# Other buffers and banks for the last element's layers 1 to 3, and a list of positions on 8 elements per partition

## The chip, the cores and the metric

The kernel runs on one core of one Trainium2 chip. The metric is the device time of one execution in microseconds. Three runs of the kernel before took 14069.84, 14073.2 and 14090.67 us; the median is 14073.2 us.

## The reference, cut to what matters

Sixteen independent elements, each with 1024 nodes, 64 features and an adjacency matrix of 1024 by 1024, pass through four residual layers:

```python
h = jnp.maximum(_layernorm(x, axis=-1), 0.0)
x = x + _L0_gnn_ref(h, adj, nodemask, W1, b1, W2, b2)   # dilated neighbours, three quantiles of their features, MLP
h = jnp.maximum(_layernorm(x, axis=-1), 0.0)
x = x + _L1_gnn_ref(h, adj)                             # (adj + I) @ h / row sum
h = jnp.maximum(_layernorm(x, axis=-1), 0.0)
x = x + _L2_gnn_ref(h, adj, ...)                        # attention, 8 heads of 64; adj is a bias on the scores
h = jnp.maximum(_layernorm(x, axis=-1), 0.0)
x = x + _L3_gnn_ref(h, adj, weight, bias)               # adj @ (h @ W) + b
```

In layer 2, with `g0` and `g1` per row, the attention is

```python
attn = g0 * (q @ k.T * SCALE) + g1 * adj
out = softmax(attn) @ v @ W_proj.T + b_proj
```

Layer 0 needs, for each node and feature, order statistics over the node's neighbours. Everything is in float32 at the interface.

## The kernel before

All loops are unrolled when the program is built. A setup builds constants in a scratch pool (`scr`), among them `rev`, the numbers 0 to 1023, each with its ten bits reversed, in float16: an iota over N = 1024 columns, the same on every partition, then ten pairs of VectorE operations (L137 and L141), a cast (L143) and a write to DRAM (L145). It is read back, 128 partitions by 1024, once for every two elements, when `ranks` turns the record of a sorting network back into ranks (L528).

After the scratch pool is closed, the working pool is opened. Before the first element's layer 0 starts, its ranks and its dilated neighbours are made (`background(0)`).

The main stage is the generator `picks`: for each of 16 elements 96 steps (8 groups of features, 2 halves of the nodes, 6 order statistics). Each step has three wide compare and multiply operations on VectorE (L735, L737, L739) and matmuls with the selection tables on TensorE. Between them stands the next element's preparation. Layers 1 to 3 of an element (`rest`) can start only when its layer 0 is over, so they are interleaved with the layer 0 of the next element: every step of `picks` gives a credit of 0.42, and a piece of layers 1 to 3 is traced for each credit used up (`two, due`, L1148). After the last element's layer 0 no picks are left; the last loop of the function (L1153) lets layers 1 to 3 of the last element run alone, with what is left of layer 3 of the element before.

Instructions run on each engine in one order that is settled when the program is built. It need not be the order of the code: `adjoining` keeps a set of matmuls together, and the instructions of a layer can be placed ahead of earlier code where they are ready.

Buffers are kept by tags. In SBUF: `a4` (4 buffers of 4 KB a partition; layer 0's compares), `tb` (6; the tables cum, c1, c0), `q4` (2), `hT` (1; layer 0's sum z), `b4` (2; `s` of layer 2, one per head, and h2), `bt` (2; transposed blocks of layers 1 and 2, and the loads of layer 3), `adj` (3; rows of the adjacency matrix, 512 KB a load), `kT`, `qT`, `v2` (1 each). In PSUM every tag has two banks: `pa`, `pc`, `pb`, and `sp`, which is one tile of two banks.

Layer 1, for each of 8 blocks of 128 rows: load `ad`, row sums on ScalarE, transpose the block in `chunk_cols` (TensorE into `pcols`, a bank of `pb`; ScalarE copies it to `aT` in `bt`), write `aT` to DRAM for layer 3, multiply by h (`weighted`, banks of `pb`), divide and add.

Layer 2, for each of 4 pairs of heads: projections into kT, qT and v by way of `pb`; then for each of 8 row blocks: load `ad` and scale it on ScalarE; for each half t of the 1024 columns the scores of both heads (L1074) go into the tile `sp`, and VectorE adds them to `ad` into `s` with a running extreme `nm` (L1083); ScalarE takes the exponential in place with its sum; `chunk_cols` transposes it to `eT`; `ao` multiplies it by v (L1093), `pp` projects it (L1104), and VectorE adds both heads to the residual (L1106). pcols, ao, pp, two and po all take their turn in the two banks of `pb`.

Layer 3 reads the transposed blocks back (`aT3` in `bt`) and multiplies.

Of the kernel before, what the change touches and what calls it, by code (L numbers as in the profile page):

```python
# [8 lines left out]
F32 = mybir.dt.float32  # L9
BF = mybir.dt.bfloat16  # L10
HP = mybir.dt.float16
F8 = mybir.dt.float8e4
I32 = mybir.dt.int32
# [8 lines left out]
P = 128  # L22
# [14 lines left out]
def tile_preln_adj_stack(  # L37
# [30 lines left out]
    nc = tc.nc  # L68
# [13 lines left out]
    def a4(name, shape=(P, N), dt=F32):  # L82
        return sb.tile(list(shape), dt, tag="a4", bufs=4, name=name)
# [14 lines left out]
    def pa(name, shape=(P, 512), dt=F32):  # L98
        return ps.tile(list(shape), dt, tag="pa", bufs=2, name=name)
# [2 lines left out]
        return ps.tile(list(shape), dt, tag="pc", bufs=2, name=name)  # L102


    def b4(name, shape=(P, N), dt=F32):
        return sb.tile(list(shape), dt, tag="b4", bufs=2, name=name)

    def pb(name, shape=(P, 512), dt=F32):
        return ps.tile(list(shape), dt, tag="pb", bufs=2, name=name)

    def small(name, shape, dt=F32, bufs=3):
# [6 lines left out]
    def sc(name, shape=(P, P), dt=F32):  # L118
        return scrp.tile(list(shape), dt, name=name)
# [7 lines left out]
    identh = const.tile([P, P], HP, name="identh")  # L127
    nc.vector.tensor_copy(identh, identf)

    rev_i = sc("rev_i", (P, N), I32)  # L130
    nc.gpsimd.iota(rev_i, pattern=[[1, N]], base=0, channel_multiplier=0)
    rev_a = sc("rev_a", (P, N), I32)
    rev_b = sc("rev_b", (P, N), I32)
    nc.vector.memset(rev_a, 0)
    for b_ in range(N.bit_length() - 1):
        up = N.bit_length() - 2 - 2 * b_
# [2 lines left out]
            op1=OP.logical_shift_left if up >= 0 else OP.logical_shift_right,  # L139
        )  # L140
        nc.vector.tensor_tensor(rev_a, rev_a, rev_b, OP.bitwise_or)  # L141
    rev = sc("rev", (P, N), HP)
    nc.vector.tensor_copy(rev, rev_a)  # L143
    rev_d = dram.tile([P, N], HP, name="rev_d")
    nc.sync.dma_start(rev_d, rev)  # L145
    not_i = const.tile([P, P], BF, name="not_i")
    nc.vector.tensor_scalar(not_i, identf, -1.0, 1.0, op0=OP.mult, op1=OP.add)
# [257 lines left out]

    def chunk_cols(ad, name):

        aT = sb.tile([P, C, P], F32, tag="bt", bufs=2, name=name)
        for s in range(2):
            pt = pb("pcols", (P, 4, P))  # L410
            adjoining(
                nc.tensor.transpose(pt[:, c, :], ad[:, (4 * s + c) * P : (4 * s + c + 1) * P], identf)  # L412
                for c in range(4)
            )
            nc.scalar.copy(aT[:, 4 * s : 4 * s + 4, :], pt)  # L415
        return aT
# [65 lines left out]
    def ranks(V):  # L482

        L = N.bit_length() - 1
        F = V
        steps = []
        for l in range(L):
            for k in range(l, -1, -1):
                steps.append((l, k))
        half = N // 2

        def sides(X, l, k):  # L500

            st = 1 << (L - 1 - k)
            v = X.rearrange("p (u two s) -> p u two s", two=2, s=st)
            lo, hi = v[:, :, 0, :], v[:, :, 1, :]
            return lo, (hi[:, ::-1, :] if k == l else hi), hi

        def like(X, k):
            return X.rearrange("p (u s) -> p u s", s=1 << (L - 1 - k))

        md = dram.tile([(len(steps) + 1) // 2, P, 2, half], HP, name="md")  # L510
        for n, (l, k) in enumerate(steps):
            G = q4("sv")
            lo, hi, _ = sides(F, l, k)
            olo, _, ohi = sides(G, l, k)
            if n % 2 == 0:
                m = b2_("sm", (P, 2, half), HP)
            nc.vector.tensor_tensor(like(m[:, n % 2, :], k), lo, hi, OP.is_gt)
            nc.vector.tensor_tensor(olo, lo, hi, OP.min)
            nc.vector.tensor_tensor(ohi, lo, hi, OP.max)
            if n % 2 == 1 or n == len(steps) - 1:  # L520
                nc.sync.dma_start(md[n // 2, :, : n % 2 + 1, :], m[:, : n % 2 + 1, :])
            F = G
            yield
        vs = dram.tile([P, N], F32, name="vs_d")
        nc.sync.dma_start(vs, F)
        yield "half"
        R = b2_("rev", (P, N), HP)
        nc.sync.dma_start(R, rev_d)  # L528

        last = (len(steps) - 1) // 4  # L530

        def fetch(i):
            m = q4("sb", (P, 4, half), HP)
            w = min(4, len(steps) - 4 * i)
            for s in range(0, w, 2):
                u = min(2, w - s)
                nc.sync.dma_start(m[:, s : s + u, :], md[2 * i + s // 2, :, :u, :])
            return m

        back = [fetch(i) for i in range(last, last - 2, -1)]  # L540
        for n in range(len(steps) - 1, -1, -1):
            l, k = steps[n]
            if n % 4 == 3 or n == len(steps) - 1:
                m = back.pop(0)
            G = b2_("sr", (P, N), HP)
            lo, _, hi = sides(R, l, k)
            olo, ohi, _ = sides(G, l, k)
            d = sb.tile([P, half], HP, tag="sd", bufs=1, name="sd")
            nc.vector.tensor_tensor(like(d, k), hi, lo, OP.subtract)
            nc.vector.tensor_tensor(d, d, m[:, n % 4, :], OP.mult)  # L550
            nc.vector.tensor_tensor(olo, lo, like(d, k), OP.add)
            nc.vector.tensor_tensor(ohi, hi, like(d, k), OP.subtract)
            R = G
            if n % 4 == 0 and n >= 8:
                back.append(fetch(n // 4 - 2))
            yield
        pt = pb("pr", (P, C, P), HP)
        adjoining(
            nc.tensor.transpose(pt[:, j, :], R[:, j * P : (j + 1) * P], identh) for j in range(C)
        )  # L560
        rs = b2_("rs", (P, C, P), HP)
        nc.scalar.copy(rs, pt)
        rk = dram.tile([P, C, P], HP, name="rk_d")
        nc.sync.dma_start(rk, rs)
        yield rk, vs
# [451 lines left out]
    def layer2(b, xr):  # L1017
# [17 lines left out]
        HW = H * D  # L1035
        for pr in range(H // 2):

            kT = sb.tile([P, N], F32, tag="kT", bufs=1, name="kT")
            qT = sb.tile([P, N], F32, tag="qT", bufs=1, name="qT")
            v = sb.tile([P, C, P], F32, tag="v2", bufs=1, name="v2")  # L1040
            for t in range(NH):
                hs = slice(t * 512, (t + 1) * 512)
                both = ((kT, slice(0, D), pb("pk")), (qT, slice(D, P), pb("pq")))
# [19 lines left out]
            for i in range(C):  # L1063
                ad = adj_rows(b, i)
                act(ad, ad, AF.Copy, scale=gm[:, i, 1:2])
                sums = small("sums", [P, 2])
                eTs = []
                ss = [b4("s") for _ in range(2)]
                nms = [None, None]
                for t in range(NH):  # L1070
                    hs = slice(t * 512, (t + 1) * 512)
                    sps = ps.tile([P, 2, 512], F32, tag="sp", bufs=1, name="sp")
                    adjoining(
                        nc.tensor.matmul(  # L1074
                            sps[:, e, :], qT[e * D : (e + 1) * D, i * P : (i + 1) * P],
                            kT[e * D : (e + 1) * D, hs], start=True, stop=True,
                        )
                        for e in range(2)
                    )
                    for e in range(2):  # L1080

                        nm = small("nm", [P, 1], bufs=6)
                        nc.vector.tensor_tensor_reduce(  # L1083
                            ss[e][:, hs], sps[:, e, :], ad[:, hs], -1.0, 3.0e38 if t == 0 else nms[e],
                            op0=OP.add, op1=OP.min, accum_out=nm,
                        )
                        nms[e] = nm
                for e in range(2):
                    act(ss[e], ss[e], AF.Exp, bias=nms[e], scale=-1.0, accum_out=sums[:, e : e + 1])
                    eTs.append(chunk_cols(ss[e], "eT"))  # L1090
                ao = pb("ao", (P, P))
                adjoining(
                    nc.tensor.matmul(  # L1093
                        ao[e * D : (e + 1) * D, :], v[:, j, e * D : (e + 1) * D], eTs[e][:, j, :],
                        start=j == 0, stop=j == C - 1, tile_position=(0, e * D), skip_group_check=True,
                    )
                    for j in range(C) for e in range(2)
                )
                rs = small("rs", [P, 2])
                nc.vector.reciprocal(rs, sums)  # L1100
                aT = small("aoT", [P, P], bufs=2)
                nc.scalar.copy(aT, ao)
                pp = pb("pp", (P, 2, D))
                nc.tensor.matmul(pp, aT, wproj[:, pr], start=True, stop=True)  # L1104
                for e in range(2):
                    nc.vector.scalar_tensor_tensor(  # L1106
                        xr[:, i, :], pp[:, e, :], rs[:, e : e + 1], xr[:, i, :], op0=OP.mult, op1=OP.add
                    )
                yield 1.0
# [39 lines left out]
    for r in picks():  # L1149
        due += r  # L1150
        while due > 0.0:
            due -= next(two) or due
    for _ in two:  # L1153
        pass

# [33 lines left out]
```

## Time and profile before

| | us |
|---|---|
| median of three runs | 14073.2 |
| profiled execution, its own time | 14083.1 |
| profiled execution, span of the core | 14080.9 |
| TensorE busy, in the span | 12452.1 (88%) |
| VectorE busy | 12849.4 (91%) |
| ScalarE busy | 8198.1 (58%) |
| GpSimd busy | 25.0 (0%) |

The profiled execution has its own time, a little above the median. The span runs from the first to the last instruction of the core. Shares are over the whole span; stages with different limits lie in it, so they are read stage by stage. In the rows of a group, `out<-in` names the tiles, the count follows the x, then come the busy time, the mean duration in ns, and the time that the engine was idle just before, with what ended it. PEld is TensorE's loading of weights, which lies beside its matmuls.

### The profile page before, as it was taken

The page shows a single profiled execution, that of the slowest core. Times are in us where ns is not written, and L with a number is a line of the kernel's source. Part 1 is how long each engine was busy: PE and PEld are TensorE (multiplying, and loading weights), DVE is VectorE, ACT ScalarE, POOL GpSimd, SP SyncE. Part 2 cuts the span into 40 slices and gives each one's busy share as a digit, 9 for nine tenths or more (in the row PEclk, how much of TensorE's full clock was granted, in tenths as well). Part 3 has the DMA queues.
Part 4 walks back from the last instruction along what each step waited for, and adds up shares of the span by engine and source line. Part 5 has one row for each costly group of instructions (what it writes and reads, how often), then busy time and mean ns, then how long its engine had stood idle before and what let it go on. Part 6 is the DMA issues. An engine that isn't in the chain of part 4 may idle for free. (4 is left out here: it accounts for less than half of the span.)

```text
span 14080.9 us, 236134 instructions
## 1 busy us (share of the span) xinstructions
PE 12452.1 (88%) x94402; PEld 5955.5 (42%) x95489; DVE 12849.4 (91%) x23280; ACT 8198.1 (58%) x14170; POOL 25.0 (0%) x138
## 2 busy tenths in 40 slices
PE   1889989999899998999899998998989999999987
PEld 0224444444444444444444444444444444444444
DVE  9999999999999999999999999999989999988863
ACT  1446656566566665656566665665656566665655
POOL 0000000000000000000000000000000000000000
PEclk9999999999999999999999999999999999999999
DMA  3012121211212112121211212122121211202011
GB/s 95 28 35 65 47 82 49 77 55 51 77 47 84 49 55 71 53 79 50 70 57 55 76 49 78 49 66 66 48 76 50 71 61 53 82 25 62 26 58 55
DMA packets 478672, 838.40 MB, mean 60 GB/s; under 512 B 232448, under 2 KB 234624, under 8 KB 477568
## 3 DMA queue, kind: packets, MB, share of 16 engines
q1 hardware_dynamic: 477568, 823.24, 18.8%
q8 instruction: 747, 12.24, 0.4%
q14 instruction: 357, 2.92, 0.1%
HBM read 616.27 MB, written 206.83 MB: 58 GB/s over the span
## 5 line engine op out<-in xcount | busy, mean ns | idle before, releaser
L699 PE MATMUL pword<-valid,dw 128*128 128x512 fp8e4 x8192 | 1985.5, 385 | 141.6 <-DVE dw L665 101.3
L691 PE MATMUL pc<-valid,cw 128*128 128x512 fp8e4 x8192 | 1973.9, 381 | 26.0 <-DVE valid L479 13.9
L737 DVE TENSOR_TENSOR wa<-le,c 128x2048 f16<-128x2048 f16 x1536 | 1865.8, 1215 | 134.8 <-PE prep L751 119.6
L735 DVE TENSOR_TENSOR le<-cum,krow 128x2048 f16<-128x2048 f16 x1536 | 1863.6, 1213 | 16.5 <-PE val L751 16.4
L739 DVE TENSOR_TENSOR wb<-le,c 128x2048 f16<-128x2048 f16 x1536 | 1864.1, 1214 | 3.5 <-PE prep L751 3.3
L362 ACT ACTIVATE s<-s,nm 128x1024 f32<-128x1024 f32 x1024 | 1169.9, 1143 | 728.3 <-DVE nm L1083 727.0
L758 ACT COPY wi<-prep 128x512 f32<-128x512 f32 x1536 | 896.8, 584 | 943.3 <-PE prep L751 796.9
L362 ACT ACTIVATE hi<-pword,mid_c 128x512 f16<-128x512 f32 x1024 | 703.2, 687 | 1140.4 <-PE pword L704 1135.5
L1074 PE MATMUL sp<-kT,qT 64*128 64x512 f32 x4096 | 1168.8, 646 | 200.8 <-DVE nm L1083 192.5
L699 PEld LDWEIGHTS <-dw 128*128 128x128 bf16 x8192 | 763.5, 99 | 1262.6 <-DVE dw L665 228.0
L412 PE MATMUL pcols<-identf,s 128*128 128x128 f32 x8192 | 1156.1, 283 | 155.7 <-ACT s L362 74.7
L691 PEld LDWEIGHTS <-cw 128*128 128x128 bf16 x8192 | 764.5, 98 | 1085.4 <-issue 250.1
L412 PEld LDWEIGHTS pcols<-identf,s 128*128 128x128 f32 x8192 | 913.8, 143 | 627.1 <-ACT eT L415 238.8
L415 ACT COPY eT<-pcols 128x512 f32<-128x512 f32 x2048 | 1110.1, 593 | 85.2 <-PE pcols L412 83.3
L1093 PE MATMUL ao<-eT,v 128*64 128x128 f32 x16384 | 1079.9, 277 | 63.8 <-ACT eT L415 60.7
L751 PE MATMUL val<-le,tab 128*32 128x512 f16 x12288 | 1092.2, 388 | 47.7 <-DVE vs L779 30.4
L779 DVE SCALAR_TENSOR_TENSOR vs<-pz,vs 128x512 f32<-128x512 f32 x1536 | 1045.0, 680 | 65.4 <-PE pv L1057 14.9
L362 ACT ACTIVATE vs<-val 128x512 f32<-128x512 f32 x1536 | 927.1, 604 | 235.7 <-PE val L751 146.3
L1093 PEld LDWEIGHTS ao<-eT,v 128*64 128x64 f32 x16384 | 905.5, 137 | 317.3 <-ACT eT L415 212.6
L694 ACT CAST cum<-pc 128x512 f16<-128x512 f32 x1024 | 603.8, 590 | 719.0 <-PE pc L691 674.7
L751 PE MATMUL prep<-wb,sel_w 128*32 128x512 f16 x6144 | 642.5, 396 | 261.8 <-DVE wb L739 238.5
L362 ACT ACTIVATE c<-pword,mid_c 128x512 f16<-128x512 f32 x1024 | 711.2, 695 | 196.9 <-PE pword L681 182.7
(260 smaller groups left out, 19147.0 us busy)
## 6 DMA issues: line engine op xcount, KB each, us to landing
ad<-in_adj_dram SPq DMA_DIRECT2D x768, 512.0 KB, 3.6
adjT_d<-aT SPq DMA_DIRECT2D x128, 512.0 KB, 4.6
aT<-adjT_d SPq DMA_DIRECT2D x128, 512.0 KB, 3.7
md<-sm SPq DMA_DIRECT2D x216, 256.0 KB, 2.0
sb<-md SPq DMA_DIRECT2D x216, 256.0 KB, 2.9
rem_d<-rem SPq DMA_DIRECT2D x128, 256.0 KB, 2.0
left_d<-left SPq DMA_DIRECT2D x128, 256.0 KB, 2.6
left<-left_d SPq DMA_DIRECT2D x128, 256.0 KB, 3.8
```

Of the source, the lines that this page charges most:

```text
L362: nc.scalar.activation(out_, in_, func, **kw)
L412: nc.tensor.transpose(pt[:, c, :], ad[:, (4 * s + c) * P : (4 * s + c + 1) * P], identf)
L415: nc.scalar.copy(aT[:, 4 * s : 4 * s + 4, :], pt)
L691: nc.tensor.matmul(pc, cw[:, j, :], valid[:, j, hs], start=j == 0, stop=j == C - 1)
L699: nc.tensor.matmul(pw_, dw[:, j, :], valid[:, j, hs], start=j == 0, stop=False, skip_group_check=True)
L735: nc.vector.tensor_tensor(le, cum, bc(el.krow[q][:, None, hs], [P, 4, 512]), OP.is_le)
L737: nc.vector.tensor_tensor(wa, le, c0, OP.mult)
L739: nc.vector.tensor_tensor(wb, le, c1, OP.mult)
L751: nc.tensor.matmul(dst[32 * pp : 32 * pp + 32, :], w[pp], r[pp], start=i in (0, 3), stop=i in (2, 4), tile_position=(0, 32 * pp),)
L779: nc.vector.scalar_tensor_tensor(vs, pz, -191.0, vs, op0=OP.is_equal, op1=OP.mult)
L1074: nc.tensor.matmul(sps[:, e, :], qT[e * D : (e + 1) * D, i * P : (i + 1) * P], kT[e * D : (e + 1) * D, hs], start=True, stop=True,)
L1093: nc.tensor.matmul(ao[e * D : (e + 1) * D, :], v[:, j, e * D : (e + 1) * D], eTs[e][:, j, :], start=j == 0, stop=j == C - 1, tile_position ...
```

## The change

A list `alone` is empty while `picks` runs and gets an entry just before the last loop. From then on (the last element's layers 1 to 3, and what is left of layer 3 of the element before) tiles are taken from other tags:

- `b4` (s, h2) takes from `a4`, with 4 buffers in place of 2;
- `chunk_cols` puts the transposed blocks into `tb`, with 6 buffers in place of 2;
- `pb` takes from `pa` for everything but `pcols`, which keeps the two banks of `pb`;
- kT, qT and v of the odd pairs of heads take from `q4` (two buffers) and `hT`;
- the scores of the second half of the columns go into two tiles of `pc`, those of the first stay in `sp`.

In the setup, `rev` is made as 8 numbers on each of 128 partitions, written to DRAM as 1024 numbers in a row, and read back with that row repeated for 128 partitions.

```diff
--- before.py
+++ after.py
@@ -102,10 +102,14 @@
         return ps.tile(list(shape), dt, tag="pc", bufs=2, name=name)
 
 
+    alone = []
+
     def b4(name, shape=(P, N), dt=F32):
-        return sb.tile(list(shape), dt, tag="b4", bufs=2, name=name)
+        return a4(name, shape, dt) if alone else sb.tile(list(shape), dt, tag="b4", bufs=2, name=name)
 
     def pb(name, shape=(P, 512), dt=F32):
+        if alone and name != "pcols":
+            return pa(name, shape, dt)
         return ps.tile(list(shape), dt, tag="pb", bufs=2, name=name)
 
     def small(name, shape, dt=F32, bufs=3):
@@ -127,10 +131,10 @@
     identh = const.tile([P, P], HP, name="identh")
     nc.vector.tensor_copy(identh, identf)
 
-    rev_i = sc("rev_i", (P, N), I32)
-    nc.gpsimd.iota(rev_i, pattern=[[1, N]], base=0, channel_multiplier=0)
-    rev_a = sc("rev_a", (P, N), I32)
-    rev_b = sc("rev_b", (P, N), I32)
+    rev_i = sc("rev_i", (P, C), I32)
+    nc.gpsimd.iota(rev_i, pattern=[[1, C]], base=0, channel_multiplier=C)
+    rev_a = sc("rev_a", (P, C), I32)
+    rev_b = sc("rev_b", (P, C), I32)
     nc.vector.memset(rev_a, 0)
     for b_ in range(N.bit_length() - 1):
         up = N.bit_length() - 2 - 2 * b_
@@ -139,9 +143,9 @@
             op1=OP.logical_shift_left if up >= 0 else OP.logical_shift_right,
         )
         nc.vector.tensor_tensor(rev_a, rev_a, rev_b, OP.bitwise_or)
-    rev = sc("rev", (P, N), HP)
+    rev = sc("rev", (P, C), HP)
     nc.vector.tensor_copy(rev, rev_a)
-    rev_d = dram.tile([P, N], HP, name="rev_d")
+    rev_d = dram.tile([P, C], HP, name="rev_d")
     nc.sync.dma_start(rev_d, rev)
     not_i = const.tile([P, P], BF, name="not_i")
     nc.vector.tensor_scalar(not_i, identf, -1.0, 1.0, op0=OP.mult, op1=OP.add)
@@ -405,7 +409,10 @@
 
     def chunk_cols(ad, name):
 
-        aT = sb.tile([P, C, P], F32, tag="bt", bufs=2, name=name)
+        aT = (
+            tb(name, (P, C, P), F32) if alone
+            else sb.tile([P, C, P], F32, tag="bt", bufs=2, name=name)
+        )
         for s in range(2):
             pt = pb("pcols", (P, 4, P))
             adjoining(
@@ -525,7 +532,7 @@
         nc.sync.dma_start(vs, F)
         yield "half"
         R = b2_("rev", (P, N), HP)
-        nc.sync.dma_start(R, rev_d)
+        nc.sync.dma_start(R, rev_d.rearrange("(o p) c -> o (p c)", o=1).to_broadcast([P, N]))
 
         last = (len(steps) - 1) // 4
 
@@ -1035,9 +1042,13 @@
         HW = H * D
         for pr in range(H // 2):
 
-            kT = sb.tile([P, N], F32, tag="kT", bufs=1, name="kT")
-            qT = sb.tile([P, N], F32, tag="qT", bufs=1, name="qT")
-            v = sb.tile([P, C, P], F32, tag="v2", bufs=1, name="v2")
+            if alone and pr % 2:
+                kT, qT = q4("kT"), q4("qT")
+                v = sb.tile([P, C, P], F32, tag="hT", bufs=1, name="v2")
+            else:
+                kT = sb.tile([P, N], F32, tag="kT", bufs=1, name="kT")
+                qT = sb.tile([P, N], F32, tag="qT", bufs=1, name="qT")
+                v = sb.tile([P, C, P], F32, tag="v2", bufs=1, name="v2")
             for t in range(NH):
                 hs = slice(t * 512, (t + 1) * 512)
                 both = ((kT, slice(0, D), pb("pk")), (qT, slice(D, P), pb("pq")))
@@ -1069,10 +1080,14 @@
                 nms = [None, None]
                 for t in range(NH):
                     hs = slice(t * 512, (t + 1) * 512)
-                    sps = ps.tile([P, 2, 512], F32, tag="sp", bufs=1, name="sp")
+                    if alone and t % 2:
+                        sps = [pc_("sp") for _ in range(2)]
+                    else:
+                        sp = ps.tile([P, 2, 512], F32, tag="sp", bufs=1, name="sp")
+                        sps = [sp[:, e, :] for e in range(2)]
                     adjoining(
                         nc.tensor.matmul(
-                            sps[:, e, :], qT[e * D : (e + 1) * D, i * P : (i + 1) * P],
+                            sps[e], qT[e * D : (e + 1) * D, i * P : (i + 1) * P],
                             kT[e * D : (e + 1) * D, hs], start=True, stop=True,
                         )
                         for e in range(2)
@@ -1081,7 +1096,7 @@
 
                         nm = small("nm", [P, 1], bufs=6)
                         nc.vector.tensor_tensor_reduce(
-                            ss[e][:, hs], sps[:, e, :], ad[:, hs], -1.0, 3.0e38 if t == 0 else nms[e],
+                            ss[e][:, hs], sps[e], ad[:, hs], -1.0, 3.0e38 if t == 0 else nms[e],
                             op0=OP.add, op1=OP.min, accum_out=nm,
                         )
                         nms[e] = nm
@@ -1150,6 +1165,7 @@
         due += r
         while due > 0.0:
             due -= next(two) or due
+    alone.append(True)
     for _ in two:
         pass
```

## The prediction

> **What bounds the kernel now.** I read the slices of the page first, to find where the bound changes; then the busy time by stages; then, inside the last stage, the waits and one iteration of the timeline; last the groups of VectorE in the setup.
>
> The slices of the page:
> ```profile
> PE   1889989999899998999899998998989999999987
> DVE  9999999999999999999999999999989999988863
> PEclk9999999999999999999999999999999999999999
> ```
> One slice is 352 us. VectorE (DVE) is full from the first slice to slice 37, TensorE (PE) nearly so from slice 2 on. Slice 1 has VectorE alone at 9: nothing else works there, so what VectorE spends in the setup is on the path. In slices 39 and 40 VectorE falls to 6 and 3 and TensorE to 8 and 7: nothing is full there.
>
> Busy time by stages (columns: stretch, length, then busy us of PE, PEld, DVE, ACT, POOL, granted clock, DMA share, GB/s). The bounds are mine: the first compare of layer 0 stands near 350, its last near 13,620; the first score of the last element's layer 2 at 13,721, its last product at 14,040.
> ```profile
> 352.00:12800.00 12448.00, 11300.49 (x85717) 5341.04 (x86732) 11711.17 (x20905) 7423.94 (x12822) 20.09 (x112) 0.98 0.19 59
> 13622.00:13722.00 100.00, 74.08 (x522) 53.99 (x520) 32.22 (x110) 40.39 (x80) 1.06 (x7) 0.74 0.41 134
> 13722.00:14041.00 319.00, 241.49 (x1924) 153.60 (x1924) 111.19 (x352) 192.99 (x335) 0.00 (x0) 0.96 0.16 49
> 14041.00:14081.00 40.00, 26.30 (x168) 21.30 (x168) 6.50 (x21) 5.98 (x14) 0.00 (x0) 0.54 0.34 110
> 13842.21:13859.76 17.55, 13.41 (x118) 8.62 (x117) 6.95 (x22) 11.56 (x20) 0.00 (x0) 1.00 0.21 61
> ```
> The third row is layer 2 of element 15 alone: TensorE works 241.5 of 319 us, ScalarE 193, VectorE 111, so 77.5 us of TensorE's time are holes. The last row is two of its 32 row blocks: 8.78 us each, of which TensorE needs 6.7, ScalarE 5.8 and VectorE 3.5.
>
> Who waits in that stage (13,737 to 14,041; waiter, releaser, total us, times, longest):
> ```profile
> DVE s L1083 <- PE sp L1074: 68.3, 33, 5.8
> DVE s L1083 <- PE pcols L412: 47.9, 54, 2.1
> PE sp L1074 <- DVE nm L1083: 35.6, 32, 1.5
> ```
> and from the timeline of one block:
> ```profile
> 13846.96 1.13 PE L1074 MATMUL sp<-kT,qT 64*128 64x512 f32 x4 [1.30 <-DVE nm L1083]
> 13848.02 1.09 PE L412 MATMUL pcols<-identf,s 128*128 128x128 f32 x8
> 13849.15 0.69 DVE L1083 CUSTOM_DVE_ANT_0 s<-sp,ad 128x512 f32<-128x512 f32 x1 [0.44 <-PE pcols L412]
> 13850.59 0.69 DVE L1083 CUSTOM_DVE_ANT_0 s<-sp,ad 128x512 f32<-128x512 f32 x1 [0.74 <-PE pcols L412]
> 13851.35 1.13 PE L1074 MATMUL sp<-kT,qT 64*128 64x512 f32 x4 [0.79 <-DVE nm L1083]
> ```
> The scores of the next block are ready at 13848.1, but VectorE may write them into `s` only once the transposes (pcols) have read the last block's `s`: `s` has two buffers, one per head. And the second half of the scores (13851.35) waits until VectorE has emptied the first, as `sp` is one pair of banks. So the blocks hang in a loop: transposes, VectorE, scores, VectorE, exponential, transposes. No engine bounds this stage; two buffers do.
>
> The setup's VectorE groups before 39.3 us:
> ```profile
> L141 DVE TENSOR_TENSOR rev_a<-rev_a,rev_b 128x1024 int32<-128x1024 int32 x10 | 12.1, 1214 | 0.0
> L137 DVE TENSOR_SCALAR rev_b<-rev_i 128x1024 int32<-128x1024 int32 x10 | 6.8, 676 | 0.0
> ```
> Half of VectorE's first 39 us is this list of positions, and no wait stands before either group.
>
> **What the Trainium skill says.** "VectorE: DVE Perf Modes", section "The TRN2 errata — SBUF-src ops pay a fixed extra latency per instruction": an operation pays a fixed cost plus its elements, (N+151)/0.96 ns for a 32-bit tensor_tensor. That is 1.224 us at 1024 elements and 0.166 us at 8; the trace has 1.214 for the first and 0.17 us for L391's 128x8 operation: agreed. "PSUM — Partial Sum Buffer", section "Summary: rules for kernel authors": to read PSUM while a matmul runs, the matmul must target a different bank (8 banks in its "Specifications (TRN2)"). The trace agrees: scores wait 35.6 us for VectorE's reads. The kernel's tags hold 2+2+2+2 banks, and the tail uses four, pb's two and sp's two. "TensorE: Matmul & The Clock Gate", section "What's actually happening": after an idle window of about 3.4 us the clock halves. The stage rows show 0.74 and 0.54 where TensorE has gaps, 0.96 in layer 2.
>
> **The change part by part**, against the profiled execution: span 14080.9, its own time 14083.1, which is 9.9 over the median of the runs shown, 14073.2. The differences below are carried over to that median.
>
> (a) Positions on 8 elements. Removed on VectorE: a memset 0.91, ten times 1.214 + 0.676, a cast 0.68: 20.5 us. Operations follow each other 0.07 to 0.08 us before the last one's end (1.214 long, 1.14 apart), so 22 of them occupied 18.8 us. Added: 22 operations of 0.15 to 0.17; a dependent one starts 0.20 after the last (44.68, 44.88, 45.08), 4.4 us for all if nothing lay between, but other small setup work does, at 0.07 to 0.13 each; I take 2.3. Net 16.5 us, bounds 14 and 18. Is it on the path? mk_u's load (35.04) and x's (35.42) are issued after the scratch is given up, and the norm starts at 39.29, so all shifts left; from 80 to 300 us VectorE is busy 207.8 of 220 us, so the shift lives on. GpSimd's iota shrinks as well (0.98 us), beside VectorE. The write of the list becomes 2 KB in pieces of 16 bytes instead of 256 KB, and each of the eight reads now repeats one row of 2 KB for 128 partitions, still 256 KB. A read lands in 2.0 to 5.9 us and no one is seen waiting for it; seven of eight lie under compares. Twice as slow would cost at most one exposed read, 3 us; I take 0.
>
> (b) From 13,622 to 13,722: rest of element 14's layer 3, then layer 1 of element 15. Layer 1's transposed blocks share the two `bt` buffers with layer 3's loads: the first transposes wait until 13,669.9, though its first `ad` blocks were there before. With tb's six buffers, and matrix products in other banks than the transposes, they fit into TensorE's 26 us of holes. Layer 1 takes 3.29 us per block, of which transposes are 1.14; eight are 9.1 us. I take 8; bounds 0 (the two 0.5 MB moves per block, at 224 GB/s in 13,650 to 13,700, are the limit anyway) and 15.
>
> (c) Layer 2. `s` gets four buffers, transposed blocks six, ao, pp and projections two banks of their own (pa), the second half of the scores the pc banks. Waits for pcols (47.9 on VectorE) and for nm (35.6 on TensorE) lose their cause. What is late next: TensorE itself with 6.7 us per block, and ScalarE with 5.8, whose queue also holds `ad`'s scaling, which waits for its load (13 times, 9.9 us); a transposed group has only two banks and must be copied out by ScalarE. The main stage runs TensorE at 11300/12448 = 91% with more other work to fill with; I take 88%: 241.5/0.88 = 274 us instead of 319, a gain of 45. Bounds: 95% gives 254, a gain of 65; 80% gives 302, a gain of 17.
>
> (d) kT, qT and v of odd pairs in other buffers: the next pair's projections (5.5 us per pair) can fill holes; that is inside (c)'s 88%. Nothing is added to any queue: the same matmuls, copies and loads.
>
> (e) Final layer 3, 40 us: `bt` and the number of banks for two and po stay, one block takes 3.01 us before and after. 0.
>
> Sum: 16.5 + 8 + 45 = 69.5. 14083.1 − 69.5 = 14013.6; against the median 14003.7: I say **14004**.
>
> **Rivals.** (1) ScalarE's order becomes the bound: its 193 us of work is in one queue, and a scale waiting for `ad` holds back copies that TensorE needs. Then 80%: gain 16.5 + 8 + 17 = 41.5, 14032. For it: the 13 waits for `ad`. Against: three `ad` buffers, and a load of 3.6 us in a block of over 7. (2) Tail nothing: the buffers free the waits, but the loop closes elsewhere, at the two pcols banks, so blocks stay near 8.7 us; only (a) remains: 14057. Against it: the transposes need 4 × 0.56 us of 8.8. (3) Tighter: 95%, clock full in (b): 14073 − 16.5 − 12 − 65 = 13980. (4) Slower: engine order is planned over the whole program (layer 1's L1000 of element 15 runs at 13,613.7, before the last compares), and a setup shorter on VectorE alone shifts the plan of the 12.4 ms of main stage. There VectorE waits 12448 − 11711 = 737 us; 9% more waits eats the gain, 13% (98 us) makes it slower by more than can be told. At 16% (118 us): 14073 − 70 + 118 = 14121. Against it: the sixteen elements repeat one pattern, and the setup ends long before it.
>
> **How the numbers follow.** Main case 0.55 (14004; its own range 13988 to 14020), rival 1 0.20, rival 2 0.08, rival 3 0.08, rival 4 0.09. A measurement of this kernel tells 0.2% (28 us) from no change. Faster: main, 1 and 3: 0.83; same: rival 2, 0.08; slower: rival 4, 0.09. The range reaches from rival 3 with (a) and (b) at their ends, 13975, over rival 1 to near rival 2, 14052.
>
> **What would show it.** (a): the first norm (L376) at 22 to 24 us instead of 39.3. (b): layer 1's first transposes before 13,660 less the shift. (c): 7.3 to 7.8 us per row block, no wait of `s` for pcols, scores of the next block ahead of this one's transposes; TensorE at 88% in the stage. Wrong if the block stays over 8.3 us, if ScalarE's waits for `ad` grow beyond 20 us, or if VectorE's idle time in the main stage moves by more than 30 us.

## The result, and the profile after

The changed kernel takes 13998.0 us (median of five runs, 13994.3 to 14014.4) against 14073.2 us before (five runs); the ratio is 0.9946, 95% interval 0.9932 to 0.9961. It is faster by 75 us. The profiled executions lie 88.3 us apart in span (14080.9 and 13992.6): the one of before was 9.9 us over its median, the one of after 3.7 us under its own.

The slices of the page after:

```profile
PE   1889999999899999999899998999989999999998
DVE  9999999999999999999999999999989999988873
PEclk9999999999999999999999999999999999999998
```

TensorE (PE) now reads 9 up to the last slice but one, where it read 8 and 7 before; VectorE reads 8, 7 and 3 in slices 38 to 40, nearly the 8, 6 and 3 of before. So the tail has become TensorE's.

The stages of the changed kernel (columns as before: stretch, length, busy us of PE, PEld, DVE, ACT, POOL, granted clock, DMA share, GB/s):

```profile
331.00:12800.00 12469.00, 11450.15 (x86905) 5358.82 (x86907) 11732.27 (x20947) 7441.23 (x12851) 20.07 (x112) 0.98 0.19 59
13598.00:13697.00 99.00, 74.87 (x520) 54.68 (x520) 32.81 (x110) 40.90 (x80) 1.06 (x7) 0.72 0.44 146
13697.00:13953.00 256.00, 239.76 (x1930) 156.48 (x1927) 111.98 (x353) 188.39 (x336) 0.00 (x0) 1.00 0.20 61
13953.00:13993.00 40.00, 26.32 (x168) 21.34 (x168) 6.21 (x20) 5.98 (x14) 0.00 (x0) 0.53 0.25 86
13728.20:13743.10 14.90, 13.81 (x117) 9.05 (x116) 7.12 (x23) 11.69 (x22) 0.00 (x0) 1.00 0.22 73
```

Layer 2 of the last element (third row) has the same work, 240 us of TensorE, in 256 us instead of 319: its holes shrank from 77.5 to 16 us. Two row blocks (last row) take 14.90 us instead of 17.55. The stage ahead of it (second row) and the final layer (fourth) are as long as before.

To set the kernels side by side, I cut each trace at four instructions: the first and the last compare of layer 0 (`le`), the first score `sp` of the last element's layer 2, and the last layer's norm. All values in us:

| kernel | first compare | main stage | last compare to first score | layer 2 | final layer |
|---|---|---|---|---|---|
| before | 348.1 | 13264.5 | 108.1 | 320.4 | 39.8 |
| after | 331.1 | 13257.9 | 107.6 | 256.2 | 39.8 |

So 17.0 us come from the setup, 64.2 from layer 2, 0.5 from the stage between, none from the final layer. The 6.6 us of the main stage come to nothing, as the experiments will show.

The setup's groups after, VectorE before 22.4 us:

```profile
L145 DVE TENSOR_TENSOR rev_a<-rev_a,rev_b 128x8 int32<-128x8 int32 x10 | 1.6, 161 | 0.0
L141 DVE TENSOR_SCALAR rev_b<-rev_i 128x8 int32<-128x8 int32 x10 | 1.6, 160 | 0.0
```

The twenty operations have gone from 18.9 us to 3.2.

Waits in layer 2 after (13,713 to 13,952; waiter, releaser, total us, times, longest):

```profile
DVE s L1098 <- PE sp L1089: 43.7, 44, 5.8
...
ACT ad L366 <- DMA ad<-in_adj_dram: 11.5, 14, 1.5
...
PE pp L1119 <- ACT aoT L1117: 9.4, 18, 0.8
DVE s L1098 <- PE pcols L419: 6.9, 22, 0.3
...
PE sp L1089 <- DVE nm L1098: 1.7, 3, 0.6
```

VectorE's wait for the transposes fell from 47.9 to 6.9 us, TensorE's for `nm` from 35.6 to 1.7. The largest wait left on TensorE is 9.4 us for the copy of ao. TensorE in one block of the changed kernel, from its timeline:

```profile
13728.20 1.13 PE L1089 MATMUL sp<-kT,qT 64*128 64x512 f32 x4
13729.25 1.96 PE L1108 MATMUL ao<-eT,v 128*64 128x128 f32 x30
13731.15 1.09 PE L419 MATMUL pcols<-identf,s 128*128 128x128 f32 x8
13732.79 0.49 PE L1119 MATMUL pp<-wproj,aoT 128*128 128x128 f32 x2 [0.55 <-ACT aoT L1117]
13733.20 1.13 PE L1089 MATMUL sp<-kT,qT 64*128 64x512 f32 x4
13734.26 1.09 PE L419 MATMUL pcols<-identf,s 128*128 128x128 f32 x8
13735.29 0.43 PE L1108 MATMUL ao<-eT,v 128*64 128x128 f32 x2
```

One gap of 0.55 us in 7.45 us, and scores (sp) of a later block on either side of this block's transposes.

### The profile page after: what moved, and what is told of

Read it like the earlier page. It is cut to its first block, busy times and chain, and to the rows that moved or that the text cites. A ratio compares the mean times of both kernels' runs of the same rounds, so it can differ in the third digit from the quotient of the medians.

```text
span 13992.6 us, 237180 instructions
## 1 busy us (share of the span) xinstructions
PE 12582.7 (90%) x95489; PEld 5964.7 (43%) x95489; DVE 12831.9 (92%) x23280; ACT 8194.5 (59%) x14170; POOL 24.1 (0%) x138
## 4 chain that ended last, share of the span: by engine, by line
DVE 29%; PE 24%; ACT 5%; issue 3%; DMA 1%; SPq 0%; DVEq 0%; ACTq 0%
DVE wa L744 4%; PE pword L706 4%; DVE wb L746 4%; DVE le L742 4%; DVE s L1098 4%; PE ao L1108 3%; PE pc L698 3%; PE pcols L419 2%; ACT s L366 2%; DVE vs L786 2%; PE prep L758 2%; PE agg L792 2%; DVE bit L773 1%; PE sp L1089 1%; PE val L758 1%
## 5 line engine op out<-in xcount | busy, mean ns | idle before, releaser
L742 DVE TENSOR_TENSOR le<-cum,krow 128x2048 f16<-128x2048 f16 x1536 | 1864.4, 1214 | 16.7 <-PE val L758 16.5
```

Source lines behind the costliest of these rows:

```text
L742: nc.vector.tensor_tensor(le, cum, bc(el.krow[q][:, None, hs], [P, 4, 512]), OP.is_le)
```

## The experiments

Twelve kernels, each compared with the kernel before and cut at the same four instructions. All stages in us. The four kernels with one run were timed beside one run of the kernel before, 14058.0; the kernel before of the others had medians of 14074.2 to 14075.0.

| kernel | first compare | main stage | to first score | layer 2 | final layer | median of its runs |
|---|---|---|---|---|---|---|
| setup alone | 332.0 | 13265.2 | 107.0 | 320.1 | 40.2 | 14058.1 |
| tail alone | 348.6 | 13268.8 | 109.1 | 256.6 | 39.7 | 14014.1 |
| s in two buffers | 331.4 | 13272.1 | 107.7 | 254.6 | 39.8 | 14001.4 |
| scores in sp alone | 332.1 | 13256.0 | 108.9 | 274.6 | 39.7 | 14010.2 |
| everything in pb | 330.2 | 13237.1 | 107.5 | 273.3 | 39.7 | 13989.6 (one run) |
| transposed blocks in two buffers | 330.7 | 13258.3 | 107.1 | 254.7 | 39.8 | 13993.4 (one run) |
| one kT, qT, v | 331.6 | 13258.5 | 107.9 | 256.2 | 39.8 | 13996.1 (one run) |
| pa alone | 330.8 | 13251.4 | 107.4 | 362.8 | 39.8 | 14093.9 (one run) |
| banks alone | 334.3 | 13258.8 | 106.8 | 254.4 | 39.8 | 13996.1 |
| SBUF buffers alone | 332.4 | 13255.8 | 104.1 | 289.2 | 39.7 | 14026.1 |
| s and sp both old | 332.7 | 13251.4 | 108.2 | 361.2 | 39.7 | 14100.0 |
| next block's product ahead | 331.7 | 13253.5 | 96.0 | 254.9 | 29.3 | 13971.7 |

### The two halves of the change

The setup alone: the kernel before with

```diff
-    rev_i = sc("rev_i", (P, N), I32)
-    nc.gpsimd.iota(rev_i, pattern=[[1, N]], base=0, channel_multiplier=0)
+    rev_i = sc("rev_i", (P, C), I32)
+    nc.gpsimd.iota(rev_i, pattern=[[1, C]], base=0, channel_multiplier=C)
...
-        nc.sync.dma_start(R, rev_d)
+        nc.sync.dma_start(R, rev_d.rearrange("(o p) c -> o (p c)", o=1).to_broadcast([P, N]))
```

> The kernel before with the list of positions alone changed (8 per partition, read back as one repeated row); the tail's buffers as before. Theory 1 (the setup's VectorE time lies on the path and the rest is only shifted): first compare at 331 us instead of 348, main stage from first to last compare 13258 to 13265 us, layer 2 of the last element 320 us, span 17 to 24 us shorter. Theory 2 (a shorter setup rearranges the planned order of the main stage): the main stage moves by more than 10 us either way.

Its first compare stands at 332.0, 16.1 us earlier than before, and no other stage moved by more than 1.1 us. Its ratio to before is 0.9989 (0.9980 to 0.9997). Theory 1 holds; the setup's gain is carried to the end and rearranges nothing.

The tail alone: the changed kernel with the old list of positions put back.

> The changed kernel with the old list of positions (1024 per partition). Theory 1: first compare at 348 us, main stage within 7 us of the kernel before's 13264.5, gap from last compare to first score of layer 2 108 us, layer 2 256 us: 64 us less than before in all. Theory 2 (the tail's tags also move the main stage, where the 6.6 us came from): main stage 13258 and 70 us less.

Layer 2 took 256.6 us, the main stage 13268.8; ratio 0.9955 (0.9940 to 0.9970). The tail's tags have no part in the 6.6 us of the main stage. Over all kernels of this study, which trace the same main stage, it lasted between 13237 and 13272 us: its scatter is larger than 6.6, and a kernel's median inherits it.

### Undoing one part of the tail

The score buffers `s`:

```diff
-        return a4(name, shape, dt) if alone else sb.tile(list(shape), dt, tag="b4", bufs=2, name=name)
+        return sb.tile(list(shape), dt, tag="b4", bufs=2, name=name)
```

> The changed kernel, but s and h2 keep the tag with two buffers. Theory 1 (two locks, s and the score banks, each enough to hold the loop): VectorE waits for the transposes again for 40 us or more, layer 2 takes 290 to 320 us instead of 256. Theory 2 (the banks were the whole matter, s only followed): layer 2 stays under 270 us.

Layer 2 took 254.6 us. My theory fell: with the second score banks in place, the two buffers of `s`, whose wait I had read as half of the lock, cost nothing. The waits of VectorE in layer 2 of this kernel (13,727 to 13,965):

```profile
DVE xr L1121 <- PE pp L1119: 59.3, 27, 5.1
DVE s L1098 <- PE pcols L419: 42.7, 53, 1.4
DVE s L1098 <- PE sp L1089: 17.5, 3, 5.8
```

VectorE still waits 42.7 us for the transposes, nearly the 47.9 of before, in a stage that is 66 us shorter. The wait is real, but VectorE has only 108 us of work in 255; my reading is that it can wait there and still be in time for TensorE.

The second pair of score banks:

```diff
-                    if alone and t % 2:
+                    if False:
                         sps = [pc_("sp") for _ in range(2)]
```

> The changed kernel, but both halves of the scores use the one tile sp of two banks. Theory 1 (two locks): TensorE waits for VectorE's nm again for some 30 us, layer 2 takes 280 to 300 us. Theory 2 (s was the whole matter; with four s buffers the planner fills the wait for the banks with other matmuls): layer 2 stays under 265 us.

274.6 us, 18 more, between the two figures: the banks count, but for less than a third of the gain. TensorE waited 13.2 us for `nm` in this layer 2 (13,697 to 13,972), not 30. Where the 18 us lie shows in the timeline, from the start of one block's `pp` to the next: in the middle of a pair of heads the blocks follow each other every 7.1 us, no slower than the 7.5 us of the changed kernel; the last two of each of the first three pairs take 12.6 us instead of 9.1, and the rest lies mostly at the start and the end of the layer.

The banks of pb:

```diff
-        if alone and name != "pcols":
-            return pa(name, shape, dt)
```

> The changed kernel, but ao, pp, the projections and two and po stay in the two banks of pb with pcols. With s in two buffers layer 2 still took 254.6 us, so my first theory of the wait at s fell. Theory 3 (the lock is pb: transposes can't start until ao and pp have left its banks, and s waits for those transposes): layer 2 at 290 us or more. Theory 4 (the lock is in the transposed blocks' two buffers): layer 2 under 265 us here.

273.3 us: again 17 us, between the two theories. TensorE's transposes wait 21.9 us for ScalarE's copies here (13,675 to 13,948), a wait that isn't among those of the changed kernel's layer 2. The two buffers of transposed blocks:

```diff
-        aT = (
-            tb(name, (P, C, P), F32) if alone
-            else sb.tile([P, C, P], F32, tag="bt", bufs=2, name=name)
-        )
+        aT = sb.tile([P, C, P], F32, tag="bt", bufs=2, name=name)
```

> The changed kernel, but transposed blocks stay in the tag with two buffers, shared with layer 3's loads. Theory 4 (two buffers of transposed blocks hold the next block's copies until the product ao is over): layer 2 at 285 us or more. Theory 3 (pb): layer 2 at 256 to 262 us. For the gap between last compare and first score: the transposes of layer 1 wait for layer 3's loads as before, so 108 us if the gap's end is set by layer 1's own chain, over 112 us if the six buffers had gained something there.

254.7 us in layer 2: nothing lost. The stage before it took 107.1 us, no longer than with six buffers, so those had gained nothing there either. And one kT, qT and v:

```diff
-            if alone and pr % 2:
+            if False:
                 kT, qT = q4("kT"), q4("qT")
```

> The changed kernel with kT, qT and v in one buffer each for all pairs of heads. The trace of the changed kernel has the projections right after the last product of the pair before, with TensorE hardly idle, so both theories expect layer 2 at 255 to 259 us; if the second set of buffers does matter, 10 us more.

256.2 us, as expected, and the order of TensorE's instructions is the same one by one: the projections of the next pair aren't moved ahead although the buffers allow it.

### Which parts do it together

No single undo had cost more than 18 of 64 us. So I went from the other side. Only pa, with `s`, the transposed blocks, kT, qT, v and sp as they were:

> The new list of positions and, of the tail's changes, only this one: everything but pcols goes from pb to pa. Two buffers of s, two of transposed blocks, one kT, qT, v, scores in sp alone. Theory 3: this takes most of the gain, layer 2 at 272 to 285 us (the 18 us of the second score banks are missing). Theory 4: layer 2 at 300 us or more.

362.8 us: 42 us slower than before. Theory 4's figure covers it, but neither theory had a layer slower than the old one, and theory 4's cause had already fallen with the undo of the transposed blocks. TensorE in a block of this kernel:

```profile
13837.58 1.13 PE L1086 MATMUL sp<-kT,qT 64*128 64x512 f32 x4 [1.31 <-DVE nm L1095]
13838.64 1.09 PE L416 MATMUL pcols<-identf,s 128*128 128x128 f32 x8
13840.02 0.66 PE L416 MATMUL pcols<-identf,s 128*128 128x128 f32 x4 [0.29 <-ACT eT L419]
13840.61 0.43 PE L1105 MATMUL ao<-eT,v 128*64 128x128 f32 x2
13840.97 0.66 PE L416 MATMUL pcols<-identf,s 128*128 128x128 f32 x4
13842.63 1.96 PE L1105 MATMUL ao<-eT,v 128*64 128x128 f32 x30 [1.00 <-ACT eT L419]
13844.52 1.13 PE L1086 MATMUL sp<-kT,qT 64*128 64x512 f32 x4
```

The next block's second half of the scores (13844.52) stands behind the whole product ao in every block. In the kernel before it stood ahead of ao in every second block:

```profile
13851.35 1.13 PE L1074 MATMUL sp<-kT,qT 64*128 64x512 f32 x4 [0.79 <-DVE nm L1083]
13852.41 1.97 PE L1093 MATMUL ao<-eT,v 128*64 128x128 f32 x32
```

My reading, which no run tests apart: with a bank free for it, ao was planned earlier, and now waits for its copies with the scores behind it. From the waits of this kernel's layer 2:

```profile
PE sp L1086 <- DVE nm L1095: 40.3, 30, 1.5
PE ao L1105 <- ACT eT L419: 32.4, 24, 2.7
```

Two readings were left: the pair of `s` and sp, or the two transposed blocks that ao waits for. The kernel with all the banks and none of the SBUF buffers (the undos of `s`, of the transposed blocks and of kT, qT, v together):

> The new list of positions and the tail's PSUM changes (pa for all but pcols, the second half of the scores in pc); s, transposed blocks, kT, qT and v in their old SBUF buffers. Each single undo cost 0 (s, transposed blocks, kT/qT/v) or 17 to 18 us (banks). Theory 5 (the banks are what counts, and SBUF buffers matter only where the banks fail): layer 2 at 254 to 265 us. Theory 6 (s and the transposed blocks stand in for each other, so undoing both closes the loop again): 285 us or more.

254.4 us, ratio to before 0.9942 (0.9929 to 0.9956): the whole gain. The kernel with the SBUF buffers and none of the banks (the undos of sp and of pb together):

> The new list of positions and the tail's SBUF changes (four s, six transposed blocks, second kT, qT, v); all PSUM banks as before. Theory 5: the two bank losses add, 256 + 17 + 18, layer 2 at 285 to 300 us, or more if they multiply. Theory 6: under 275 us.

289.2 us, ratio 0.9966 (0.9952 to 0.9979): about half the gain of layer 2, 31 of 64 us; the two bank losses add up (256 + 17 + 18 = 291). And `s` and sp both old, the rest as changed:

> The changed kernel with s in two buffers and the scores in the one tile sp; pa, six transposed blocks and the second kT, qT, v stay. Alone, the first undo cost nothing and the second 18 us; with pa alone (also two transposed blocks) layer 2 took 362.8 us. Theory 5a (s and sp are one lock in two places: either one free lets the next block's scores in, both tied stop them): layer 2 at 320 to 365 us. Theory 6 (in the kernel with pa alone it was the two transposed blocks that held the product ao, 32 us of waits): layer 2 at 275 to 290 us.

361.2 us, ratio 1.0018 (1.0011 to 1.0024), with the six transposed blocks in place; TensorE's wait of ao for its copies is 33.4 us, where it was 32.4 with two. So the transposed blocks weren't the matter. `s` and the score banks are two ways out of one place: with either in plenty the next block's scores get in (254.6 with the banks, 274.6 with the buffers); with neither, layer 2 is slow, and slower still when ao has banks of its own (320.4 before, 361.2 here). The second score banks alone, with everything else as before, weren't tried.

### A version that beats both

In the changed kernel's final layer, each block goes product, copy, second product:

```profile
13967.71 1.98 PE L986 MATMUL two<-aT,hid 128*64 128x128 f32 x16
13970.10 0.69 PE L995 MATMUL po<-ident,aoT 128*128 128x64 f32 x2 [0.42 <-ACT aoT L993]
13970.72 1.98 PE L986 MATMUL two<-aT,hid 128*64 128x128 f32 x16
13973.12 0.69 PE L995 MATMUL po<-ident,aoT 128*128 128x64 f32 x2 [0.42 <-ACT aoT L993]
```

Each po waits 0.42 us for the copy, with nothing between. The last kernel takes the next block's product ahead of it (layer 1 likewise), and gives po and layer 3's loads other tags:

```diff
-        po = pb("po", (P, D))
+        po = (pc_ if alone else pb)("po", (P, D))
...
-            po = weighted(aT, hid)
-            nc.vector.tensor_tensor(xr[:, i, :], xr[:, i, :], po, OP.add)
+            part = weighted(aT, hid)
+            if ahead is not None:
+                add(*ahead)
+            ahead = (i, part)
...
-            aT = sb.tile([P, C, P], F32, tag="bt", bufs=2, name="aT3")
+            aT = (
+                tb("aT3", (P, C, P), F32) if alone
+                else sb.tile([P, C, P], F32, tag="bt", bufs=2, name="aT3")
+            )
```

> The changed kernel, and in the part after the last compare, layers 1 and 3 issue the next block's product two before this block's po, po has banks of its own (pc), and layer 3's loads use the six tb buffers. In the changed kernel a block of the last layer 3 takes 3.01 us, two 1.98 at the lower clock, then a copy, then po. If that chain is what sets it: 1.5 to 2.5 us per block, the last stage 40 us down to 28 to 35, the gap from last compare to first score 107.6 down to 95 to 103, all else equal: 10 to 25 us less. If loads set it: no change in either stage.

The final layer took 29.3 us instead of 39.8, the stage between compares and scores 96.0 instead of 107.6: 22 us in all. The median is 13971.7 us (13966.5 to 13981.3), ratio to before 0.9927 (0.9913 to 0.9940), against 13998.0 for the changed kernel. Its final layer:

```profile
13947.94 3.68 PE L986 MATMUL two<-aT,hid 128*64 128x128 f32 x32 [0.68 <-ACT hid L1151]
13951.55 0.69 PE L998 MATMUL po<-ident,aoT 128*128 128x64 f32 x2
13952.17 1.77 PE L986 MATMUL two<-aT,hid 128*64 128x128 f32 x16
...
13957.02 1.09 PE L986 MATMUL two<-aT,hid 128*64 128x128 f32 x16
13958.04 0.43 PE L998 MATMUL po<-ident,aoT 128*128 128x64 f32 x2
```

No po waits any more, and after two blocks the clock rises: `two` takes 1.09 us instead of 1.98. Which of the three edits carries how much wasn't tried apart.

## Why the prediction was right, and where not

**Total.** Predicted 14004, measured 13998.0; predicted gain 69.5 us, measured 75.2 in the medians and 81.7 by the stages that moved with the change (17.0 + 0.5 + 64.2). Two of its terms were off in opposite ways, (b) by 7.5 us too much and (c) by 19 us too little, and the medians lie 6.5 us nearer to each other than the stages say. That the total came within 6 us is in part luck.

**(a) The setup: right.** 16.5 predicted, 17.0 in the profile, 16.1 with this part alone. The first norm stands at 22.4 us; I had written 22 to 24. One read of the repeated row was waited for, 1.0 us, inside the bound of 3.

**(b) From the last compare to the first score: wrong.** The step that failed is "they fit into TensorE's 26 us of holes", taken as 8 us. The transposes did come earlier, and the stage stayed. TensorE's timeline of the changed kernel:

```profile
13625.76 1.14 PE L419 MATMUL pcols<-identf,ad 128*128 128x128 f32 x8
...
13648.19 1.98 PE L986 MATMUL two<-aT,h 128*64 128x128 f32 x16
...
13671.93 0.43 PE L995 MATMUL po<-ident,aoT 128*128 128x64 f32 x2 [0.42 <-ACT aoT L993]
13679.16 1.89 PE L407 MATMUL pt<-identf,h 128*64 128x128 f32 x8 [6.80 <-DVE h L399]
```

The first block of transposes ran 36.8 us after the last compare (13625.8 − 13589.0), where before it ran 57.3 us after it. But layer 1's products (13648.2) start only after all of layer 3's, a chain of some 3.0 us per block. I had counted holes on an engine that was in a chain. What layer 1 saved by having transposes done early was lost in layer 3: layer 3's last `two` starts 56.2 to 57.5 us after the last compare in the kernels with pa (the last experiment aside), 51.1 to 54.6 in those with pb. Layer 1's last `po` starts after 82.9 us in the changed kernel and after 82.4 with the setup alone, whose tail is the old one. With the three edits of the last experiment, which loosen the chain, the stage lost 11.6 us. The 104.1 us of the kernel with the SBUF buffers alone are mostly the clock: its pv takes 1.94 us, where the changed kernel's takes 3.57.

The reading beneath (b) was wrong too: not the two `bt` buffers held the transposes back, but the banks. The first of layer 1's transposes, with six transposed blocks and everything in pb, and with two transposed blocks and pa:

```profile
13621.68 1.91 PE L417 MATMUL pcols<-identf,ad 128*128 128x128 f32 x8
13625.63 1.13 PE L416 MATMUL pcols<-identf,ad 128*128 128x128 f32 x8
```

That is 54.4 us after the last compare (13567.3) in the first, and 36.6 us (13589.0) in the second.

**(c) Layer 2: right in kind, the size too small.** The mis-sized term is TensorE's share, 88%, taken a little below the main stage's 91%: it became 239.8/256 = 93.7%, so 64 us and not 45. My own mark of 7.3 to 7.8 us per block held (7.45), but two blocks from the middle don't stand for the layer: 32 times (8.78 − 7.45) is 43 of the 64 us. From `pp` to `pp`, the second pair of heads took 81.7 us before and 64.7 after: the first five steps after its first `pp` went from 42.5 to 36.3, the last two from 16.9 to 9.1, and the step from the pair before, with the projections in it, from 22.3 to 19.3. More than half of that pair's gain lies at its ends.

The reading beneath it was half wrong: "two buffers do" named `s` and sp as two locks. They are one, with two keys, and the third part, pb, that I only mentioned, weighs as much as sp when either is undone alone (17 and 18 us).

**(d) kT, qT, v: right.** Nothing, shown by the same order of instructions without them. **(e) Final layer: right**, 39.8 in both, though the reason that I gave (the same buffers and banks) hid that one could gain 10 us there.

**Rivals.** ScalarE's waits for `ad` grew only from 9.9 to 11.5 us, and TensorE's share is far from rival 1's 80%. Rival 2 is excluded by 64 us. Rival 3 had layer 2's size, 65 us, but its full clock in the stage before didn't come (0.72 there). Rival 4, a rearranged main stage, isn't seen: with the setup alone the main stage took 13265.2 us against 13264.5, and VectorE's idle time from the first compare to 12,800 is 737 us before and after. That a part of the tail can be planned worse and become slower does happen, but elsewhere: in the kernel with pa alone, in layer 2.

## What to carry to other kernels

A long wait in the table names a candidate, not a cost: VectorE's 42.7 us on the transposes stayed while the stage lost 66 us. Where a buffer change comes as a bundle, undo its parts singly and together; here five parts, of which two (the banks) make the whole gain, three are idle beside them, and one of the two alone makes the kernel slower than it was. Idle beside the others isn't idle: without the second score banks, the four buffers of `s` are worth 87 us of layer 2 (361.2 against 274.6). Giving a product other banks changes the order of work, so it can lose as well as win. And a block from the middle of a loop doesn't show what is lost at the loop's ends.

## What the runs showed of the hardware

The clock of TensorE stayed low in the changed kernel's final layer although TensorE was busy 2.59 of every 3.01 us there: with one gap of 0.42 us per block `two` took 1.98 us in all eight blocks (granted clock 0.50 from 13,967.7 to 13,988). In the last kernel, without the gaps, it came to 1.09 us after some 6 us of work, and a block took 1.39 us instead of 3.01: 1.6 us less, where the gap itself was 0.42.

The length of the gap alone doesn't settle it. In the kernel before, the first blocks of the last element's layer 1 have the same gap, but 4.3 us of work between two gaps (13674.31 to 13678.62), and there the clock rose:

```profile
13674.31 0.69 PE L988 MATMUL po<-ident,aoT 128*128 128x64 f32 x2 [0.42 <-ACT aoT L986]
13674.79 1.91 PE L412 MATMUL pcols<-identf,ad 128*128 128x128 f32 x8
13676.64 1.98 PE L979 MATMUL two<-aT,h 128*64 128x128 f32 x16
13679.03 0.43 PE L988 MATMUL po<-ident,aoT 128*128 128x64 f32 x2 [0.42 <-ACT aoT L986]
13679.30 1.14 PE L412 MATMUL pcols<-identf,ad 128*128 128x128 f32 x8
```

It also falls without a long gap: with the setup alone, TensorE was busy for 6.05 of the 9.3 us from 13,636.1 to 13,645.4, at full clock and with no idle stretch over 1.21 us, and after that `two` took 1.98 us. No idle stretch like the 3.4 us that the prediction went by stands before this fall. What rule the clock follows isn't settled by these runs.
